# Turning the value products of three attention stages: values as weights in 32-column tiles, exponentials streamed, key sums from a block of ones

## The chip, the core and the metric

One Trainium2 chip, one core. The metric is the device time of one execution of the whole program, in microseconds (us). The program computes a four-layer decoder for 128 sequences of 64 tokens with 128 features, all in float32; what is changed lies in three of its twelve steps.

The engines are named as in the profile: PE multiplies matrices (its weight loads are listed apart, as PEld), DVE is the vector engine, ACT the scalar engine, POOL the general engine, SP starts DMAs. A matmul holds one operand (the weights, or stationary operand) and streams the other; the result goes to PSUM, a small memory of eight banks, from which DVE and ACT read.

## What is computed

The three steps are multi-head attentions with 16 heads of 8 features over 64 keys. The first, cut to what matters:

```python
qh = (q @ W_q).reshape(B, S, 16, 8); kh = (k @ W_k).reshape(...); vh = (v @ W_v + b_v).reshape(...)
scores = jnp.einsum('bihd,bjhd->bhij', qh, kh) * scale
keep = (j < i) | (i == 0) & (j == 0)
probs = jax.nn.softmax(jnp.where(keep, scores, -jnp.inf), axis=-1)
attn = jnp.einsum('bhij,bjhd->bihd', probs, vh).reshape(B, S, 128)
return attn @ W_o + b_o
```

The second adds a bias that falls with the distance of query and key (and has no bias on the values); the third masks by an input matrix, and has biases on the values and on the output. A layer normalization of x plus the result follows each. Two other attentions share the code and keep their old form: one with differential heads, one with padded keys.

## The kernel before

**Chunks.** All tokens stay in SBUF as 16 arrays X[c] of 128x4x128: a chunk c is 512 tokens, that is 8 sequences (BPC) or 4 blocks of 128 tokens (TPC). `mha` (L1160) runs an attention step as a pipeline over the chunks. Tile pools and a scheduler decide buffers and the final order on each engine; each engine works in order.

**One chunk, in two halves hf of 4 sequences.** `project` makes q and k, with features on partitions, and `expanded` copies of them in which all heads but one are zero (L1185 on ACT, L1187 on POOL and DVE). `project_v` (L1204) makes the values, with keys on partitions, and ACT copies them to VX (L1223). `scores` (L1225) multiplies queries and keys into four PSUM banks s_ps, adds the mask with matmuls (L1471, L1602), and DVE takes the maximum over the keys, four reductions m of 128x512 (L1243). `split_maxima` (L1249) splits the maxima into two bf16 parts hl, and `maxima` (L1256) turns them on PE into mT. `weights` (L1264) computes the same scores the other way round, keys on partitions, into four banks t_ps (L1273), adds the mask (L1473, L1476, L1608) and the maxima by a matmul with mT (L1285), and ACT takes the exponential into e (L1292): 128 partitions (two parities of heads by 64 keys) by 4 groups of 512 columns.

**The value products.** `values` (L1296) takes e as the weights, 64 columns for one head pair and sequence, and streams 18 columns of VX: 8 value features for each of the two heads of a pair, and two columns that hold one for the keys of the one or the other, so that the sum of the exponentials comes out beside the output (L1310). 32 such matmuls make one half. The result has queries on partitions. DVE inverts the 32 sums (L1315) and multiplies (L1324) into o, 128x4x128.

**After it.** The output projection needs features on partitions, so `transposed` (L328) turns o with four PE transposes and an ACT copy, which also adds the values' bias where there is one (L335); then four matmuls with W_o, an addition on DVE (L407), and the layer normalization (`ln_stats` L373 to L376, `rsqrt` L347 to L352, `ln_apply` L385 or L387).

**What sets the order.** The body of mha's loop (L1328 to L1363) for chunk c: `weights(c, 0)`, `load(c + 2)`, `values(c - 1, 1)`, `scores(c + 1, 0)`, the transposes of chunk c - 1, `project_v(c + 1)`, `weights(c, 1)`, `values(c, 0)`, `scores(c + 1, 1)`, `split_maxima(c + 1)`, `project(c + 2)`, the output projection of c - 1, `maxima(c + 1)`. s_ps and t_ps share a pool of five banks (psA); av_ps, oT_ps, v_ps, the q and k products, y and mT_ps share one of three (psB).

**Work put aside into the loop.** In the second step (`attn_alibi`) `rejoin` puts a row gather at each of four places of the loop: DVE copies an index column to `fat` (L1863), POOL starts an indirect DMA that adds rows to X (L1864). In the third step (`xattn_masked`) `kept` advances the planner of the last step, with matmuls, DVE and POOL work of its own. Its masks come by DMA (L1585), one of the two into a part of VX, and DVE turns them into bf16 (L1590).

**VX** are two arrays of 128x2176 for even and odd chunks. Before each attention POOL sets them to zero (L1174) and copies the ones (L1176). `cleared` uses a part of VX[0] as a source of zeros for DMAs (L2160).

Of the kernel before, what the change touches and what calls it, by code (L numbers as in the profile page):

```python
# [15 lines left out]
U8 = mybir.dt.uint8  # L16
# [6 lines left out]
P = 128  # L23
# [217 lines left out]
def tile_decoder(ctx: ExitStack, tc: tile.TileContext, a, out):  # L241
# [73 lines left out]
    def sc(n):  # L315
        return small[:, _SMALL[n][0] : _SMALL[n][1]]
# [840 lines left out]
    def rows32(t, g):  # L1157
        return t[32 * g : 32 * g + 32]

    def mha(prepare, wv, finish, mask=None, diff=False, aside=lambda c, k, seen: None):  # L1160

# [7 lines left out]
        wide_v = 2 * dh + 2  # L1169
        scale = 1.0 / math.sqrt(HD)  # L1170
        st = {}
        vxs = [v[:, : BPC * 8 * wide_v].rearrange("p (b n w) -> p b n w", b=BPC, n=8) for v in VX]
        for v in vxs:
            G.memset(v, 0.0)  # L1174
            for i in range(2):
                G.tensor_copy(v[:, :, :, 2 * dh + i], sc("vm2")[:, i : i + 1, None].to_broadcast([P, BPC, 8]))  # L1176

        def expanded(x, n, eb):

# [24 lines left out]
        def project_v(c):  # L1204
            src, vx = st[c]["src"], vxs[c % 2]
            per = dh * 8
            ps = [bank("v_ps") for _ in range(BPC * per // 512)]
            nb = 512 // per
            for b in range(BPC):
                for i in range(2):  # L1210
                    w = wv if diff else wv.rearrange("p (n i d) -> p i n d", n=8, i=2)[:, i]
                    mm(
                        ps[b // nb][i * S : (i + 1) * S, b % nb * per : (b % nb + 1) * per],
                        src[:, b * S : (b + 1) * S], w, start=True, stop=True,
                    )
            for n, v in enumerate(ps):
                for i in range(2):
                    q = slice(i * S, (i + 1) * S)
                    dst, src_ = vx[q, n * nb : (n + 1) * nb, :, i * dh : (i + 1) * dh], v[q].rearrange("p (b n d) -> p b n d", b=nb, n=8)
                    if diff and i:  # L1220
                        A.activation(dst, src_, AF.Identity, scale=nlam[q])
                    else:
                        A.copy(dst, src_)  # L1223
# [71 lines left out]

        def values(c, hf):  # L1296
            s = st[c]
            if hf == 0:
                s["o"] = work("o", (P, TPC, D))
                s["tmp"] = work("ye", (P, 2, 8, 2, 16), "dtmp") if diff else None  # L1300
            e, o, vx = s["e"][hf], s["o"], vxs[c % 2]
            ev = e.rearrange("p g (a u j q) -> p g a u j q", u=2, a=2, j=2)
            n_t = 1 if diff else 2
            for u0 in range(0, 2, n_t):
                ps = bank("av_ps")
                av = ps[:, : n_t * 8 * wide_v].rearrange("p (n w) -> p n w", w=wide_v)
                for u in range(u0, u0 + n_t):
                    for n in range(8):
                        for j in range(2):
                            mm(  # L1310
                                av[j * S : (j + 1) * S, 8 * (u - u0) + n, :], ev[:, n // 2, n % 2, u, j, :],
                                vx[:, 2 * (2 * hf + u) + j, n, :], start=True, stop=True,
                            )
                rc = sm.tile([P, 8 * n_t, 2], F32, tag=f"rc{n_t}", name="rc")
                V.reciprocal(rc, av[:, :, 2 * dh :])  # L1315
                src = av[:, :, : 2 * dh].rearrange("p n (i d) -> p n i d", i=2)
                t = 2 * hf + u0
                if diff:
                    d = s["tmp"][:, u0]
                    V.tensor_tensor(d, src, rc[:, :, :, None].to_broadcast([P, 8, 2, dh]), ALU.mult)  # L1320
                    G.tensor_tensor(o[:, t, :].rearrange("p (n d) -> p n d", n=8), d[:, :, 0, :], d[:, :, 1, :], ALU.add)
                else:
                    dst = o[:, t : t + 2, :].rearrange("p t (n i d) -> p (t n) i d", n=8, i=2)
                    return V.tensor_tensor(dst, src, rc[:, :, :, None].to_broadcast([P, 16, 2, dh]), ALU.mult).ins  # L1324

        nlam = lam_neg() if diff else None
        on, late, spread, done = range(NC), (), None, None
# [36 lines left out]
        for _ in late:  # L1364
            pass

    def out_projected(c, o, wo, bv=None, base=None, after=None, on_act=False):
        oT = transposed(o, "oT", bias=bv)
        xb = base() if base else None
        yield  # L1370
        y = bank("y")
        for t in range(TPC):
            mm(y[:, t * P : (t + 1) * P], oT[:, t * P : (t + 1) * P], wo, start=True, stop=True)
        r = added(c, y, xb)
        yield
        layernorm(c, r, on_act=on_act)
        if after:
            after(c)
# [15 lines left out]
    def attn_diff():  # L1394
# [49 lines left out]
        mha(prepare, w[:, 2, :], finish, diff=True)  # L1444
        layernorm(NC - 1, rs.pop(NC - 1))


# [38 lines left out]
    def xattn_causal():  # L1486
        w = W[4]
        cleared([(XR, 4 * P * QUADS)])
        mha(
            cross(w, None, None), w[:, 2, :],  # L1490
            lambda c, s: out_projected(c, s["o"], w[:, 3, :], bv=col("l1xbv"), base=lambda: with_bias(c, "l1xbo")),
            mask=everywhere(half[:, 128:256].rearrange("p (n h k) -> p n h k", n=2, h=1)),
        )

    def attn_alibi():
# [4 lines left out]

        def finish(c, s):
            c = order[c]
            oT = transposed(s["o"], "oT")
# [29 lines left out]
    def xattn_padded():  # L1533
# [33 lines left out]
            yield  # L1567
            layernorm(c, r)

        mha(cross(W[7], "l2xbq", "l2xbk"), W[7][:, 2, :], finish, mask=mask)  # L1570

    def xattn_masked():
        w = W[10]
# [22 lines left out]
        def mask(c, hf, s, t):  # L1596
# [12 lines left out]

        mha(  # L1610
            prepare, w[:, 2, :],
            lambda c, s: out_projected(c, s["o"], w[:, 3, :], bv=col("l3xbv"), base=lambda: with_bias(c, "l3xbo"), on_act=c > 11),
            mask=mask, aside=kept,
        )

# [541 lines left out]

    def cleared(stores):

        z = VX[0][:, BPC * 8 * 18 : BPC * 8 * 18 + D]  # L2160
        G.memset(z, 0.0)
        for x, n in stores:
            for o in range(0, n, 16 * P):
# [52 lines left out]
```

## Time and profile before

| | us |
|---|---|
| median of 8 runs (3368.92 to 3395.17) | 3379.93 |
| the profiled execution | 3382.01 |
| its span, first to last instruction | 3378.9 |

| engine | busy us | share of the span |
|---|---|---|
| PE | 2897.4 | 86% |
| PEld | 2099.2 | 62% |
| DVE | 2035.5 | 60% |
| ACT | 1620.3 | 48% |
| POOL | 1535.5 | 45% |

The mean granted clock of PE is 0.915. In the page's list of groups, L1310 is the costliest on PE: its matmuls are busy for 348.2 us and its weight loads for 328.3 us. Busy times overlap, since matmuls are pipelined: a mean of 217 ns for one does not mean one per 217 ns.

Three views are used further on. The view of stretches has a row for each stretch: from and to, length, busy time and number of instructions, granted clock, share of the DMA engines, GB/s. The timeline has a row for instructions of one kind in succession: start, duration from the first to the last, engine, line, operation, output and inputs, array tile or shape, number; in brackets the idle time before it and what ended that. The list of groups has busy time and mean duration, then the idle time before and its causes. A f32 matmul shows as two records, a weight load and a matmul each, as it takes two passes.

### The profile page before, as it was taken

The page shows a single profiled execution, that of the slowest core. Times are in us where ns is not written, and L with a number is a line of the kernel's source. Part 1 is how long each engine was busy: PE and PEld are TensorE (multiplying, and loading weights), DVE is VectorE, ACT ScalarE, POOL GpSimd, SP SyncE. Part 2 cuts the span into 40 slices and gives each one's busy share as a digit, 9 for nine tenths or more (in the row PEclk, how much of TensorE's full clock was granted, in tenths as well). Part 3 has the DMA queues.
Part 4 walks back from the last instruction along what each step waited for, and adds up shares of the span by engine and source line. Part 5 has one row for each costly group of instructions (what it writes and reads, how often), then busy time and mean ns, then how long its engine had stood idle before and what let it go on. Part 6 is the DMA issues. An engine that isn't in the chain of part 4 may idle for free. (4 is left out here: it accounts for less than half of the span.)

```text
span 3378.9 us, 110606 instructions
## 1 busy us (share of the span) xinstructions
PE 2897.4 (86%) x46690; PEld 2099.2 (62%) x46690; DVE 2035.5 (60%) x7300; ACT 1620.3 (48%) x3150; POOL 1535.5 (45%) x1543
## 2 busy tenths in 40 slices
PE   5898868998998899978788899998998669988993
PEld 3788845665666677845565677773443337766882
DVE  3732357766777666443355565667888876663345
ACT  2443346755554565322344545553545556643443
POOL 3555545234555444234455354556666224353244
PEclk9999988999999899788788889999998899996996
DMA  4577721000001000014510000000000000011684
GB/s 121 153 193 228 227 59 37 14 8 3 3 3 43 27 4 4 6 37 113 139 14 13 3 5 4 4 10 3 1 1 7 4 5 18 18 32 42 185 247 121
DMA packets 191633, 182.22 MB, mean 54 GB/s; under 512 B 30176, under 2 KB 166624, under 8 KB 191136
## 3 DMA queue, kind: packets, MB, share of 16 engines
q1 hardware_dynamic: 160688, 136.66, 13.9%
q0 software_dynamic: 20224, 32.28, 4.2%
q8 instruction: 366, 6.00, 0.7%
q10 hardware_dynamic: 10224, 6.22, 0.6%
q14 instruction: 131, 1.07, 0.1%
HBM read 132.34 MB, written 42.73 MB: 52 GB/s over the span
## 5 line engine op out<-in xcount | busy, mean ns | idle before, releaser
L1243 DVE TENSOR_REDUCE m<-s_ps 128x8 f32<-128x512 f32 x640 | 397.5, 683 | 201.4 <-PE s_ps L1471 100.3
L1292 ACT ACTIVATE e<-t_ps 128x512 f32<-128x512 f32 x640 | 329.5, 599 | 175.7 <-PE t_ps L1285 175.3
L1310 PE MATMUL av_ps<-vx,e 128*64 128x18 f32 (+1 forms) x10240 | 348.2, 217 | 14.4 <-issue 13.1
L1310 PEld LDWEIGHTS av_ps<-vx,e 128*64 128x64 f32 x10240 | 328.3, 142 | 36.6 <-issue 28.9
L792 ACT ACTIVATE hT<-h_ps,aux 128x256 f32<-128x256 f32 x496 | 204.3, 471 | 254.5 <-PE h_ps L790 137.6
L1187 POOL TENSOR_SCALAR eb<-qT,small 128x512 f32<-128x512 f32 x80 | 131.7, 1646 | 381.2 <-ACT qT L970 170.1
L1273 PE MATMUL t_ps<-eb,kT 32*64 32x128 f32 x10240 | 289.0, 287 | 7.2 <-DVE m L1243 3.3
L1235 PE MATMUL s_ps<-eb,qT 32*64 32x256 f32 x5120 | 249.9, 423 | 48.1 <-ACT e L1292 23.4
L825 POOL DMA_INDIRECT got<-l_rout,fat x192 | 192.7, 1004 | 210.6 <-DVE r L835 95.8
L790 PE MATMUL h_ps<-ebT,rw 128*128 128x256 f32 x992 | 245.9, 392 | 25.4 <-DVE ebT L778 10.1
L803 PEld LDWEIGHTS yg<-rw,hT 128*128 128x128 f32 x1984 | 244.0, 193 | 15.4 <-ACT hT L792 6.1
L803 PE MATMUL yg<-rw,hT 128*128 128x128 f32 x1984 | 246.8, 277 | 5.4 <-ACT hT L792 4.0
L1273 PEld LDWEIGHTS t_ps<-eb,kT 32*64 32x64 f32 x10240 | 203.3, 133 | 76.4 <-DVE m L1243 26.5
L387 POOL TENSOR_SCALAR x<-xb,lnmv,ln_y 128x128 f32<-128x128 f32 x200 | 157.3, 798 | 159.8 <-DVE ln_y L352 159.8
L765 POOL DMA_INDIRECT aux<-in_x_dram,rat x156 | 159.7, 1024 | 143.9 <-issue 55.4
L1315 DVE RECIPROCAL rc<-av_ps 128x32 f32<-128x32 f32 (+1 forms) x192 | 61.7, 321 | 268.6 <-PE av_ps L1310 261.5
L790 PEld LDWEIGHTS h_ps<-ebT,rw 128*128 128x128 f32 x992 | 183.7, 195 | 53.8 <-DVE ebT L778 13.7
L804 DVE TENSOR_TENSOR yo<-yg,aux 128x256 f32<-128x256 f32 x124 | 52.4, 422 | 265.9 <-PE yg L803 87.7
L1235 PEld LDWEIGHTS s_ps<-eb,qT 32*64 32x64 f32 x5120 | 126.6, 141 | 101.9 <-ACT e L1292 38.7
L1185 ACT ACTIVATE eb<-qT,small 128x512 f32<-128x512 f32 x160 | 106.8, 715 | 128.7 <-POOL qT L1412 123.8
L1187 POOL TENSOR_SCALAR eb<-kT,small 128x512 f32<-128x512 f32 x80 | 145.6, 1820 | 21.5 <-ACT kT L972 11.4
L1968 PE MATMUL ye_ps<-w_l2f,box 128*128 128x512 f32 x256 | 135.8, 649 | 0.0
(517 smaller groups left out, 6444.9 us busy)
## 6 DMA issues: line engine op xcount, KB each, us to landing
rw<-in_l0w_dram SPq DMA_DIRECT2D x78, 512.0 KB
rw<-in_l3w_dram SPq DMA_DIRECT2D x46, 512.0 KB
l_rout<-yo SPq DMA_DIRECT2D x124, 128.0 KB
aux<-xd SPq DMA_DIRECT2D x46, 128.0 KB
aux<-in_l0b_dram SPq DMA_DIRECT2D x78, 66.0 KB
xd<-vx SPq DMA_DIRECT2D x5, 1024.0 KB
plan<-xr ACTq DMA_DIRECT2D x18, 256.0 KB
yr<-plan SPq DMA_DIRECT2D x18, 256.0 KB
```

Source lines behind the costliest of these rows:

```text
L387: (V if on_dve else G).tensor_scalar(X[c][:, t, :], r[:, t, :], mv[:, t, 0:1], y[:, t : t + 1], ALU.subtract, ALU.mult)
L765: s.gather = G.indirect_dma_start(out=eb[:, i, :], out_offset=None, in_=x[:, :], in_offset=bass.IndirectOffsetOnAxis(ap=at[:, i : i + 1], ...
L790: s.pe = mm(ps[:, j * GR : (j + 1) * GR], w1[:, (k + j) * P : (k + j + 1) * P], ebT, start=True, stop=True)
L792: s.act_ins = A.activation(hT[k + j], ps[:, j * GR : (j + 1) * GR], s.act, bias=v[:, k + j : k + j + 1])
L803: s.pe = mm(y[:, i * P : (i + 1) * P], hT[k][:, i * P : (i + 1) * P], w2[:, k, :], start=(k == 0), stop=(k == FK - 1))
L825: s.gather = G.indirect_dma_start(out=got[i][k][:, t, :], out_offset=None, in_=s.rout[b][:, :], in_offset=bass.IndirectOffsetOnAxis(ap=at[ ...
L1187: ins = (G if h == 2 else V).tensor_scalar(dst, x, mine, None, ALU.mult)
L1235: mm(ps[g][j * S : (j + 1) * S, u * 256 : (u + 1) * 256].rearrange("p (h k) -> p h k", h=4), rows32(s["q"], g)[:, b], rows32(s["eb"], g)[: ...
L1243: last = V.tensor_reduce(s["m"][:, g, 2 * hf : 2 * hf + 2, :].rearrange("p t h -> p (t h)"), ps[g].rearrange("p (n k) -> p n k", k=S), AX. ...
L1273: mm(ps[g][i * S : (i + 1) * S].rearrange("p (a u j q) -> p a u j q", u=2, a=2, j=2)[:, :, u, j, :], rows32(s["k"], g)[:, b], rows32(s["eb ...
L1292: last = A.activation(e[:, g, :], ps[g], AF.Exp, scale=scale)
L1310: mm(av[j * S : (j + 1) * S, 8 * (u - u0) + n, :], ev[:, n // 2, n % 2, u, j, :], vx[:, 2 * (2 * hf + u) + j, n, :], start=True, stop=True,)
```

## The change

The new form, `turned_values`, is used with `flat=True`, in the causal, the biased and the masked attention; the other two pass `flat=False` and stay as they were.

```diff
-        vxs = [v[:, : BPC * 8 * wide_v].rearrange("p (b n w) -> p b n w", b=BPC, n=8) for v in VX]
...
+        if flat:
+            vxs = [v[:, : BPC * 4 * 48] for v in VX]
+            key_sums = VX[1][:, 2048:2096]
+            G.memset(key_sums, 0.0)
+            for v in vxs:
+                G.memset(v, 0.0)
             for i in range(2):
+                G.tensor_copy(key_sums[:, 16 + i * dh : 16 + (i + 1) * dh], sc("vm2")[:, i : i + 1].to_broadcast([P, dh]))
...
+                    if flat:
+                        A.copy(
+                            vx[q].rearrange("p (m x r) -> p m x r", x=3, r=16)[:, :, 0::2, i * dh : (i + 1) * dh],
+                            v[q].rearrange("p (m x d) -> p m x d", x=2, d=dh),
+                        )
+                        continue
...
+        def turned_values(s, hf, vx):
+
+            if hf == 0:
+                s["oT"] = work("oT")
+            ps = bank("av_ps")
+            av, total = ps[:, :256], ps[:, 256:]
+            for a_ in range(2):
+                for g in range(4):
+                    mm(
+                        total[32 * g : 32 * g + 32, :], key_sums[:, 16 - 16 * a_ : 48 - 16 * a_],
+                        s["e"][hf][:, g, a_ * 256 : (a_ + 1) * 256], start=(a_ == 0), stop=(a_ == 1), skip_group_check=True,
+                    )
+            for x in range(4):
+                for a_ in range(2):
+                    for g in range(4):
+                        at = ((4 * hf + x) * 4 + g) * 48 + 16 * a_
+                        mm(
+                            av[32 * g : 32 * g + 32, x * S : (x + 1) * S], vx[:, at : at + 32],
+                            s["e"][hf][:, g, a_ * 256 + x * S : a_ * 256 + (x + 1) * S], start=(a_ == 0), stop=(a_ == 1), skip_group_check=True,
+                        )
+            dst = s["oT"][:, hf * 256 : (hf + 1) * 256]
+            V.reciprocal(dst, total)
+            return V.tensor_tensor(dst, av, dst, ALU.mult).ins
...
+    def with_values_bias(bo, bv, wo):
+
+        ps = bank("bo_ps")
+        mm(ps[:, :D], col(bv).to_broadcast([P, P]), wo, start=True, stop=True)
+        V.tensor_tensor(row(bo), row(bo), ps[:, :D], ALU.add)
+
+    def out_projected(c, oT, wo, base=None, after=None, on_act=False):
-        oT = transposed(o, "oT", bias=bv)
...
-        used = BPC * 8 * 18
+        used = BPC * 4 * 48
+        with_values_bias("l3xbo", "l3xbv", w[:, 3, :])
...
-            m = work("t1", (P, BPC * 2 * S // 4), "mu").bitcast(U8), VX[c % 2][:, used + 512 : used + 768].bitcast(U8)
+            m = [work(n, (P, BPC * 2 * S // 4), "mu").bitcast(U8) for n in ("t1", "o")]
```

In words. The values are now the weights and the exponentials are streamed. In VX each sequence and group g of four heads has 48 columns: 16 for the first head pair (a_ = 0), 16 zeros, 16 for the second. The 32 columns from 0 or from 16 are the weights for the one or the other pair, with zeros in the place of the other, and the two products are added in PSUM. A group's output takes 32 of the 128 partitions, so the four groups fill the 128 features, and the output has features on partitions: 32 matmuls of 64 streamed columns for a half. The sums come from 8 matmuls of 256 columns with a block of ones (`key_sums`, in the same layout), so that each of the 128 output rows has its sum in the same bank, beside it. DVE inverts 128x256 sums and multiplies into oT, which the output projection takes as it is. The transposes of o and their copies are gone; the values' bias, multiplied by W_o, is added to the row of the output's bias once at the start of the step. The masks' second tile moves from VX to the buffers of tag "o", which these attentions no longer use, and the source of zeros in `cleared` moves to the end of VX[0].

More of the change, by code (lines that the diff above doesn't have):

```diff
@@ L1158, in rows32, with mha @@
         return t[32 * g : 32 * g + 32]
-    def mha(prepare, wv, finish, mask=None, diff=False, aside=lambda c, k, seen: None):
+    def mha(prepare, wv, finish, mask=None, diff=False, aside=lambda c, k, seen: None, flat=True):
         dh = 16 if diff else 8
@@ L1171, in mha @@
         st = {}
-        vxs = [v[:, : BPC * 8 * wide_v].rearrange("p (b n w) -> p b n w", b=BPC, n=8) for v in VX]
-        for v in vxs:
-            G.memset(v, 0.0)
-            for i in range(2):
-                G.tensor_copy(v[:, :, :, 2 * dh + i], sc("vm2")[:, i : i + 1, None].to_broadcast([P, BPC, 8]))
+        if flat:
[4 more added lines that the diff above has]
+                G.memset(v, 0.0)
+            for i in range(2):
+                G.tensor_copy(key_sums[:, 16 + i * dh : 16 + (i + 1) * dh], sc("vm2")[:, i : i + 1].to_broadcast([P, dh]))
+        else:
+            vxs = [v[:, : BPC * 8 * wide_v].rearrange("p (b n w) -> p b n w", b=BPC, n=8) for v in VX]
+            for v in vxs:
+                G.memset(v, 0.0)
+                for i in range(2):
+                    G.tensor_copy(v[:, :, :, 2 * dh + i], sc("vm2")[:, i : i + 1, None].to_broadcast([P, BPC, 8]))
         def expanded(x, n, eb):
@@ L1297, in values @@
             s = st[c]
+            if flat:
+                return turned_values(s, hf, vxs[c % 2])
             if hf == 0:
@@ L1365, in mha @@
             pass
-    def out_projected(c, o, wo, bv=None, base=None, after=None, on_act=False):
-        oT = transposed(o, "oT", bias=bv)
+    def with_values_bias(bo, bv, wo):
[3 more added lines that the diff above has]
+    def out_projected(c, oT, wo, base=None, after=None, on_act=False):
         xb = base() if base else None
@@ L1442, in finish @@
             rs[c] = added(c, ps)
-        mha(prepare, w[:, 2, :], finish, diff=True)
+        mha(prepare, w[:, 2, :], finish, diff=True, flat=False)
         layernorm(NC - 1, rs.pop(NC - 1))
@@ L1488, in xattn_causal @@
         cleared([(XR, 4 * P * QUADS)])
+        with_values_bias("l1xbo", "l1xbv", w[:, 3, :])
         mha(
             cross(w, None, None), w[:, 2, :],
-            lambda c, s: out_projected(c, s["o"], w[:, 3, :], bv=col("l1xbv"), base=lambda: with_bias(c, "l1xbo")),
+            lambda c, s: out_projected(c, s["oT"], w[:, 3, :], base=lambda: with_bias(c, "l1xbo")),
             mask=everywhere(half[:, 128:256].rearrange("p (n h k) -> p n h k", n=2, h=1)),
@@ L1502, in finish @@
             c = order[c]
-            oT = transposed(s["o"], "oT")
+            oT = s["oT"]
             r = with_bias(c, "l2abo")
@@ L1568, in finish @@
             layernorm(c, r)
-        mha(cross(W[7], "l2xbq", "l2xbk"), W[7][:, 2, :], finish, mask=mask)
+        mha(cross(W[7], "l2xbq", "l2xbk"), W[7][:, 2, :], finish, mask=mask, flat=False)
     def xattn_masked():
@@ L1611, in xattn_masked @@
             prepare, w[:, 2, :],
-            lambda c, s: out_projected(c, s["o"], w[:, 3, :], bv=col("l3xbv"), base=lambda: with_bias(c, "l3xbo"), on_act=c > 11),
+            lambda c, s: out_projected(c, s["oT"], w[:, 3, :], base=lambda: with_bias(c, "l3xbo"), on_act=c > 11),
             mask=mask, aside=kept,
@@ L2158, in cleared @@
     def cleared(stores):
-        z = VX[0][:, BPC * 8 * 18 : BPC * 8 * 18 + D]
+        z = VX[0][:, 2048 : 2048 + D]
         G.memset(z, 0.0)
```

## The prediction

> **What bounds the kernel now.** I read the stretches of the three stages that change, then one clean chunk of the causal stage on PE and DVE, then the same spot in the other two stages. Each attention stage runs 16 chunks, and each chunk two products of exponentials and values: A (the second half of the chunk before, L1338) and B (the first half of this one, L1348).
>
> ```profile
> 1112.00:1400.00 288.00, 275.27 (x8016) 0.99 0.02 5
> 1650.00:2005.00 355.00, 311.65 (x7902) 0.89 0.08 13
> 2760.00:3125.00 365.00, 328.69 (x8059) 0.90 0.09 27
> ```
>
> The rows are the causal, alibi and masked stages: length, PE busy time, granted clock. PE is busy 96% of the causal stage, so it looks as if only PE work counted. The chunk shows otherwise:
>
> ```profile
> 1195.85 2.05 PE L1310 MATMUL av_ps<-vx,e 128*64 128x18 f32 x64
> 1197.82 1.12 PE L1235 MATMUL s_ps<-eb,qT 32*64 32x256 f32 x32
> 1198.74 0.64 PE L1471 MATMUL s_ps<-half 32*64 32x512 bf16 x16
> 1199.31 0.65 PE L332 MATMUL oT_ps<-ident,o 128*128 128x128 f32 x4
> 1199.89 1.15 PE L1212 MATMUL v_ps<-w_l1x,ctx 128*64 128x64 f32 x32
> ```
>
> ```profile
> 1193.53 0.10 PEld L1260 LDWEIGHTS <-hl 128*128 128x128 bf16 x1 [0.65 <-DVE hl L1254]
> 1201.34 0.86 PEld L1273 LDWEIGHTS t_ps<-eb,kT 32*64 32x64 f32 x55 [0.17 <-DVE m L1243]
> ```
>
> ```profile
> 1188.30 0.36 DVE L1315 RECIPROCAL rc<-av_ps 128x32 f32<-128x32 f32 x1 [3.32 <-PE av_ps L1310]
> 1188.70 0.42 DVE L1324 TENSOR_TENSOR o<-av_ps,rc 128x256 f32<-128x256 f32 x1
> 1189.76 2.48 DVE L1243 TENSOR_REDUCE m<-s_ps 128x8 f32<-128x512 f32 x4 [0.64 <-PE s_ps L1471]
> ...
> 1197.94 0.36 DVE L1315 RECIPROCAL rc<-av_ps 128x32 f32<-128x32 f32 x1 [0.44 <-PE av_ps L1310]
> 1199.40 2.48 DVE L1243 TENSOR_REDUCE m<-s_ps 128x8 f32<-128x512 f32 x4 [0.64 <-PE s_ps L1471]
> ```
>
> Twice a chunk PE already waits for DVE: in half A for the maxima m, which free the banks that t_ps takes; in half B for hl, made of m. DVE's order in both halves is reciprocal, product, four maxima. Before the first maximum it idles 0.64 us for s_ps. That gap is all the cover that a longer reciprocal has; with the 0.08 us by which neighbouring DVE instructions overlap when neither waits (1189.76+2.48 against a next start of 1192.16), 0.72 us.
>
> **The change, part by part.** *Matmuls.* Before, 32 products stream 18 columns against 64-column weights: 1195.85 to 1197.82, 1.97 us, weight-load bound. After, 8 matmuls of 256 columns give the sums and 32 of 64 columns the values, on tiles of 32 columns, four side by side. Each f32 matmul shows as two records. s_ps has 32 such records of 256 columns on eight tiles, four rounds in 0.92 us (1197.82 to 1198.74); the sums are 16 records on four tiles, four rounds: 0.92 us. v_ps has 32 records of 64 columns on two tiles, 16 rounds in 1.08 us; the values are 64 records on four tiles, 16 rounds: at most 1.08, and 0.93 by the 58 ns between its records. Together 1.85 to 2.00 us; I take 1.87, 0.1 us less than before, on the path in both halves. That four column tiles run together is seen in the routed stage, where four products (eight records) take no longer than one's two passes and a tail:
>
> ```profile
> 1575.72 0.43 PE L1799 MATMUL hq_ps<-plan,vx 128*32 128x128 f32 x8
> ```
>
> The Trainium skill (TensorEngine Tiling (Array Packing), Performance Considerations) promises up to 4x for swapping the streamed side and tiling columns. By that rule a product would take 0.5 us, and 1.37 less than I take on 67 exposed products, and the whole would end near 3344 us. The rows above say that a round lasts as long as its streamed columns or its weight load, and that before, two tiles of 18 columns already ran side by side; after, half of every 32-column tile holds zeros, so no such factor is there to win.
>
> *Reciprocal.* It grows from 128x32 to 128x256, because the sums now stand under every output row.
>
> ```profile
> L1315 DVE RECIPROCAL rc<-av_ps 128x32 f32<-128x32 f32 x128 | 45.5, 356 | 257.8 <-PE av_ps L1310 250.8 <-remote 6.9
> L1315 DVE RECIPROCAL rc<-av_ps 128x16 f32<-128x16 f32 x64 | 16.1, 252 | 10.8 <-PE av_ps L1310 10.6
> ```
>
> Sixteen more columns cost 104 ns, 6.5 ns each, so 224 more cost 1.46 us: 1.81 us. The planner's two, of 28 and 36 columns, take 329 and 370 ns: 5.1 ns each, 1.50 us. A floor is the rate of the maxima, 621 ns for 512 columns (1.2 ns): 0.63 us. I take 1.81, whose form and operand (PSUM) are nearest.
>
> The Trainium skill has two rules here: VectorE: DVE Perf Modes, in its Walkthrough, says that the reciprocal is an iterative divide with a repeat count of 8. At the page's 0.96 GHz that would be 8.3 ns a column, 2.2 us, and the total near 3463. Its errata section's table, 120 cycles plus one per element, would give 0.39 us and no delay at all. The two rows above, 6.5 ns a column, refute the second and lie under the first.
>
> *Causal.* Each half: 1.46 less 0.72 makes m 0.74 us late; behind m on DVE stand the cast and split to hl, whose consumers are PE's transpose and then every later matmul. Less 0.1 for the matmuls: 0.64. Two halves, 15 chunks: 19 us.
>
> *Alibi.* In nine chunks a row gather follows the product. DVE copies its indices (fat), POOL starts it, and m begins only some 1.4 us after the gather's start, though by PE's timeline s_ps ended at 1816.66:
>
> ```profile
> 1815.61 0.42 DVE L1324 TENSOR_TENSOR o<-av_ps,rc 128x256 f32<-128x256 f32 x1
> 1815.95 0.15 DVE L1863 COPY fat<-pli 128x1 int32<-128x1 int32 x1
> 1817.75 2.48 DVE L1243 TENSOR_REDUCE m<-s_ps 128x8 f32<-128x512 f32 x4 [1.65 <-PE qT_ps L967]
> ```
>
> ```profile
> 1816.37 1.55 POOL L1864 DMA_INDIRECT x<-yr,fat  x1 [3.42 <-DVE fat L1863]
> ```
>
> So the idle 1.65 us is no cover: copy, gather and m all move by 1.46 in B. In A, DVE idles 5.2 us there behind ACT: nothing. 9 x 1.46 = 13; three chunks with B alone at 0.74, 2; four like causal, 8 x 0.74 = 6; matmuls -2. Sum 19. If the gather does not hold m, the 13 go.
>
> *Masked.* In eight chunks A starts behind the layernorm chain with 0.36 + 0.08 us of cover, so 1.02 late, 8 us; B has 2.2 us of idle behind the planner's matmuls: nothing. Two first chunks like causal, 3. In the last six, five products stand in back-to-back DVE work, 7. Matmuls -2. Sum 16. The transposed mask moves to tag "o", whose four loads follow the scan's release, ahead of their use by some 10 us (first t_ps 2772.55): nothing; uncovered, about one load, 2 us.
>
> *The rest.* The four oT transposes (0.58 us on PE) and ACT's copy (0.69) go, but PE then reaches t_ps earlier and waits for m longer: nothing, up to the 0.2 us it waits now. The vx copies keep 64x512 elements. The folded bias is a matmul and a 128x128 addition, twice, under 1 us each. The zeroing grows by a third of 1.06 us, against four 0.30 us copies dropped. At each stage's end the longer reciprocal stands against the dropped transposes and copy. Together +2.
>
> Sum: 19 + 19 + 16 + 2 = 56. The profiled execution took 3382.01 us (span 3378.9), 2.1 above the median 3379.93; on the median's scale 3436.
>
> **Rivals.** (1) Faster: the reciprocal costs under 0.36 + 0.72 = 1.08 us at 256 columns, which decides, and m is no later. Then matmuls gain 0.1 on some 67 exposed products (7) and dropping the transposes 0.2 on 40 chunks (8): 3365. Against it: all reciprocal rows. (2) Column tiles run only in pairs: 1.87 becomes 3.74, 1.77 more on 88 products, 155, plus 56: 3590. Against: hq_ps. (3) The delay is hidden outside causal chunks: 19 + 6 of alibi's last + 3: about 3408. For: DVE's long idle there; against: the gather's constant 1.4 us. (4) Nothing is covered, DVE's order makes all 96 products late by 1.46 less 0.1: 131, 3511. Against: the 2.2 and 5.2 us gaps. That the change doesn't do what it says is excluded by the built order: 96 products have 8 + 32 matmuls and the wide reciprocal, and the transposes are gone.
>
> **How the numbers follow.** Forecast 0.66; rivals 0.08, 0.04, 0.13, 0.09. Within the forecast, the slope of 5.1 takes 0.31 from 67 products, 21; a free gather takes 13, the planner's chunks 7: down to 3395. Low 3397; up, half of rival 4: 3475. No change is within 0.3%, about what this kernel's measurement can tell: 0.03, from the overlap of (1) and (3). Faster 0.08, slower 0.89.
>
> **What would show it.** DVE's reciprocal near 1.8 us, 96 times, DVE busy some 135 us more; no idle on DVE before m in causal; PE waiting for m and hl by 0.7 us more a half; values' records in 1.9 us; the causal stage 19 us longer with less PE busy. A reciprocal under 1.1 us, or PE gaps unchanged, would make it wrong.

## The result, and the profile after

The changed kernel takes 3396.66 us (median of 22 runs, 3385.26 to 3415.66), the kernel before 3378.37 (64 runs); the ratio is 1.0062, 95% interval 1.0047 to 1.0076. So it is slower, by 18 us where 56 were forecast, just below the forecast range. The profiled execution took 3405.45 us (span 3403.6, mean granted clock 0.927), 23.4 more than that of before.

First the stretches of PE, from the first maximum of a stage to its last. The columns are those of the prediction: from and to, length, PE busy and its instructions, granted clock, DMA share, GB/s. The rows are causal, alibi, the end of alibi (its last maxima to the padded stage's first) and masked; before:

```profile
1120.86:1379.08 258.22, 248.50 (x7471) 1.00 0.02 4
1647.53:1984.74 337.21, 296.63 (x7470) 0.89 0.09 15
1984.74:2020.93 36.19, 29.34 (x539) 0.80 0.03 8
2767.25:3081.64 314.39, 290.64 (x7551) 0.95 0.08 23
```

and after:

```profile
1118.93:1399.11 280.18, 257.19 (x7880) 0.99 0.06 17
1665.06:2001.18 336.12, 285.93 (x7884) 0.93 0.07 10
2001.18:2027.86 26.68, 23.72 (x579) 0.94 0.04 11
2775.95:3107.34 331.39, 296.04 (x7960) 0.95 0.08 21
```

Causal is 22.0 us longer (19 forecast), masked 17.0 (16 forecast). Alibi is 1.1 shorter (19 longer forecast) and its end 9.5 shorter (nothing forecast). All other stretches together are 3.7 shorter; the sum, 24.7, is the difference of the spans.

The groups of the changed kernel, with the idle time before them and its main cause:

```profile
L1258 DVE TENSOR_REDUCE m<-s_ps 128x8 f32<-128x512 f32 x640 | 396.8, 682 | 108.3 <-PE s_ps L1517 49.6
L1364 DVE RECIPROCAL oT<-av_ps 128x256 f32<-128x256 f32 x96 | 168.6, 1756 | 189.4 <-PE av_ps L1359 189.4
L1288 PEld LDWEIGHTS t_ps<-eb,kT 32*64 32x64 f32 x10240 | 214.8, 132 | 114.5 <-DVE m L1258 61.1
```

The reciprocal takes 1.756 us, 96 times (1.81 forecast). The idle time before the maxima has halved (201.4 us before): it was the cover. PE's weight loads for t_ps now wait 61.1 us for the maxima (26.5 before). DVE is busy 2169.8 us, 134 more (135 forecast).

A clean causal chunk on DVE and then on PE, start and duration of each row, in brackets the idle time and what ended it:

```profile
1205.55 1.76 DVE L1364 RECIPROCAL oT<-av_ps 128x256 f32<-128x256 f32 x1 [0.41 <-PE av_ps L1359]
1207.34 0.42 DVE L1365 TENSOR_TENSOR oT<-av_ps,oT 128x256 f32<-128x256 f32 x1
1207.68 2.47 DVE L1258 TENSOR_REDUCE m<-s_ps 128x8 f32<-128x512 f32 x4
```

```profile
1203.52 1.07 PE L1351 MATMUL av_ps<-e,vx 128*32 128x256 f32 x16
1204.41 1.08 PE L1359 MATMUL av_ps<-e,vx 128*32 128x64 f32 x64
1205.41 1.12 PE L1250 MATMUL s_ps<-eb,qT 32*64 32x256 f32 x32
```

The product is 0.89 us of sums and 1.00 of values, 1.89 together (1.87 forecast, 1.97 before). The maxima follow the product without a gap. The causal period is 18.0 to 18.8 us a chunk; before it was 16.9 in the first chunks and 17.1 to 18.2 in most later ones. Over the 13 chunks from the third on, the stage loses 16.1 us, 0.62 us a half (0.64 forecast). The excess over 19 us is in the second chunk (21.9 for 16.8), which holds two waits for instructions of 0.8 us and slower matmuls behind a wait for hl.

Half B of alibi behind a gather, where the forecast failed, on DVE and POOL:

```profile
1781.40 1.76 DVE L1364 RECIPROCAL oT<-av_ps 128x256 f32<-128x256 f32 x1 [4.07 <-PE av_ps L1359]
1783.19 0.42 DVE L1365 TENSOR_TENSOR oT<-av_ps,oT 128x256 f32<-128x256 f32 x1
1783.53 0.14 DVE L1911 COPY fat<-pli 128x1 int32<-128x1 int32 x1
1783.59 2.47 DVE L1258 TENSOR_REDUCE m<-s_ps 128x8 f32<-128x512 f32 x4
1785.98 0.87 DVE L1196 TENSOR_SCALAR eb<-qT,small 128x512 f32<-128x512 f32 x1
...
1787.48 0.57 DVE L1269 TENSOR_TENSOR hl<-m,hl 128x64 bf16<-128x64 f32 x1
```

```profile
1783.94 1.55 POOL L1912 DMA_INDIRECT x<-yr,fat  x1 [4.76 <-DVE fat L1911]
1785.01 2.30 POOL L1196 TENSOR_SCALAR eb<-qT,small 128x512 f32<-128x512 f32 x1
```

Before, the gather started first and m 1.4 us behind it, 2.53 us after the reciprocal's start. Now s_ps is done when the product ends, m starts at once, 2.19 us after the reciprocal's start, and the gather starts 0.35 us behind m. So m comes 0.34 us earlier than it did, but what follows m takes longer: from m's start to the end of hl it is 4.46 us, where it was 3.71. The same two DVE rows in the half before:

```profile
1820.15 0.48 DVE L1187 TENSOR_SCALAR eb<-qT,small 128x512 f32<-128x512 f32 x1
...
1821.25 0.21 DVE L1254 TENSOR_TENSOR hl<-m,hl 128x64 bf16<-128x64 f32 x1
```

POOL's two eb instructions take 2.30 us each beside them, where they took 1.57 and 1.79; why both engines are slower here, no run shows. From the start of the reciprocal to the end of hl it is 6.65 us, where it was 6.24: the half is 0.40 us longer, not 1.46.

### The profile page after: what moved, and what is told of

It is laid out like the page before. It is cut to its first block, busy times and chain, and to the rows that moved or that the text cites. A ratio compares the mean times of both kernels' runs of the same rounds, so it can differ in the third digit from the quotient of the medians.

```text
span 3403.6 us, 113204 instructions
## 1 busy us (share of the span) xinstructions
PE 2882.3 (85%) x48038; PEld 2029.9 (60%) x48038; DVE 2169.8 (64%) x7302; ACT 1589.1 (47%) x3102; POOL 1538.3 (45%) x1540
## 4 chain that ended last, share of the span: by engine, by line
PE 47%; DVE 31%; issue 7%; ACT 6%; POOL 5%; DMA 3%; another core or an unknown queue 1%; SPq 0%; POOLq 0%; DVEq 0%; ACTq 0%
DVE m L1258 8%; PE h_ps L790 5%; PE yg L803 5%; PE s_ps L1250 4%; PE t_ps L1288 3%; DVE oT L1364 3%; PE av_ps L1327 3%; PE av_ps L1359 2%; PE av_ps L1351 2%; PE y L1134 2%; DVE lnst L373 2%; POOL x L387 1%; PE ye_ps L2016 1%; PE t_ps L1300 1%
## 5 line engine op out<-in xcount | busy, mean ns | idle before, releaser
L1288 PE MATMUL t_ps<-eb,kT 32*64 32x128 f32 x10240 | 321.3, 287 | 25.2 <-DVE m L1258 12.8
L1364 DVE RECIPROCAL oT<-av_ps 128x256 f32<-128x256 f32 x96 | 168.6, 1756 | 189.4 <-PE av_ps L1359 189.4
L1288 PEld LDWEIGHTS t_ps<-eb,kT 32*64 32x64 f32 x10240 | 214.8, 132 | 114.5 <-DVE m L1258 61.1
L1250 PE MATMUL s_ps<-eb,qT 32*64 32x256 f32 x5120 | 241.5, 406 | 36.5 <-ACT e L1307 19.6
L1327 PE MATMUL av_ps<-vx,e 128*64 128x34 f32 (+1 forms) x4096 | 137.5, 220 | 3.7 <-issue 3.5
L1327 PEld LDWEIGHTS av_ps<-vx,e 128*64 128x64 f32 x4096 | 129.6, 140 | 12.3 <-issue 9.7
```

The costliest lines, as they stand in the source:

```text
L1250: mm(ps[g][j * S : (j + 1) * S, u * 256 : (u + 1) * 256].rearrange("p (h k) -> p h k", h=4), rows32(s["q"], g)[:, b], rows32(s["eb"], g)[: ...
L1288: mm(ps[g][i * S : (i + 1) * S].rearrange("p (a u j q) -> p a u j q", u=2, a=2, j=2)[:, :, u, j, :], rows32(s["k"], g)[:, b], rows32(s["eb ...
L1327: mm(av[j * S : (j + 1) * S, 8 * (u - u0) + n, :], ev[:, n // 2, n % 2, u, j, :], vx[:, 2 * (2 * hf + u) + j, n, :], start=True, stop=True,)
L1364: V.reciprocal(dst, total)
```

## The experiments

The runs fell on chips of two kinds. On some the kernel before takes 3360 to 3380 us, as in the result above, on others 3240; the first maximum of the first attention comes after 745 to 759 us on the former and 686 to 699 on the latter. Ratios are to the kernel before on the same chip. They are called the 3380 and the 3240 chips. Chip number 3 stands in both kinds (e5 to e8 at 3240, e13 to e16 at 3380), so whether the chips themselves differ, their machines or a state that changes with time, isn't shown.

### The long reciprocal alone, in the kernel before (e1, e15)

```diff
...
-                V.reciprocal(rc, av[:, :, 2 * dh :])
+                if wide_rc:
+                    rc = work("oT", (P, 16, 16), "rc")
+                    V.reciprocal(rc, av[:, :, 2:])
+                    rc = rc[:, :, 14:]
...
```

> The kernel before, with one thing changed: in the causal, biased and masked attentions DVE inverts 128x256 elements of av_ps where it inverted 128x32 (the 32 sums among them, which alone are used). PE's work, the transposes and the turn of the output stay as before. Theory 1 (the reciprocal's extra 1.4 us is exposed only where the scores' banks wait for DVE; behind a row gather it uses up the hold that the gather had on the maxima): causal +19 to +22 us, masked +16, the nine gather chunks of alibi about 0 in B and its last chunks +6, so +40 to +45 in all, ratio 1.012 to 1.013. Theory 2 (the prediction's: the gather moves along and holds the maxima all the same): alibi +19 to +21, in all +55 to +58, ratio 1.0165. Theory 3 (the loss comes from the new matmuls or from the instruction stream, not from DVE): within 0.3% of before.

> The kernel before with the long reciprocal alone. Theory 1 (the forecast's price of the reciprocal, 1.9%, is right in size, and what was missed is what the dropped turn gives back): 1.018 to 1.022; against the profile of before on this chip causal +17 to +20, alibi +9 to +14, masked +15 to +18. Theory 2 (the reciprocal costs less than forecast): 1.010 to 1.014.

Measured on 3380 chips: 1.0208 (1.0179 to 1.0237) and 1.0194 (1.0174 to 1.0215). The reciprocal's price in the forecast was 56 us and the 7 that the matmuls were to gain, 1.9%: right in size for the old form, and theory 1 of e15 by the total. Its place was right in part: in e15 causal is 21 us longer than in the profile of before on that chip, masked 19, alibi 12.5, and its end 9. These are rough, as the profile of e15 fell on its longest execution (3461 us, granted clock 0.901) and also has 21 us more between causal's last maxima and alibi's first, where next to nothing was changed; from the first profile of before to e1 they are 19, 10, 10 and 3.5. The total is above what any theory of e1 expected; alibi is near theory 1, though not 0 in its B halves. DVE's rows of such a half, in e1:

```profile
1674.71 1.76 DVE L1316 RECIPROCAL rc<-av_ps 128x256 f32<-128x256 f32 x1 [4.09 <-PE av_ps L1310]
...
1676.90 2.47 DVE L1243 TENSOR_REDUCE m<-s_ps 128x8 f32<-128x512 f32 x4
```

As in the changed kernel, m follows the product without a gap and no longer waits behind the gather: the gather's hold and the reciprocal do not add up.

### The changed kernel with a short reciprocal (e2), and a square of four (e9 to e12)

```diff
-            V.reciprocal(dst, total)
-            return V.tensor_tensor(dst, av, dst, ALU.mult).ins
+            rc = sm.tile([P, 32], F32, tag="rc2", name="rc")
+            V.reciprocal(rc, total[:, :32])
+            return V.tensor_tensor(..., rc[:, None, :].to_broadcast([P, 8, 32]), ALU.mult).ins
```

It inverts 32 of the 256 columns of sums and scales every query by one of these, so its outputs are not the attention's; it serves only to price the reciprocal. The square has a long or a short reciprocal, without the turn (the transposes and their copy) or with it. The turn kept as dead work, at the start of what follows each chunk's product:

```diff
+    def turned_again(oT):
+        ps = bank("oT_ps")
+        for t in range(TPC):
+            nc.tensor.transpose(ps[:, t * P : (t + 1) * P], oT[:, t * P : (t + 1) * P], ident)
+        A.copy(work("o"), ps)
```

> The changed kernel, but DVE inverts only the first 32 of the 256 columns of sums, and every query of a half is scaled by one of these 32, so the outputs of the three attentions are scaled by other queries' sums. All matmuls, the dropped transposes and the second product on DVE stay. Theory 1: without the long reciprocal m is no later than before; the matmuls' 0.1 us on some 67 exposed products (7) and what the dropped transposes give at the stages' ends (12 in the one profile) are left: 3355 to 3370 us, ratio 0.993 to 0.998; and in alibi's B halves the maxima start about 1.4 us behind the gather's start again, as before, so that alibi gains no more than in the changed kernel. Theory 2 (the gather holds the maxima however early they could start): the gather chunks of alibi are 1.4 us shorter than in the changed kernel. Theory 3 (the new matmuls cost it): still 1.004 to 1.007.

> The changed kernel with the dropped work put back as dead work: after each first half of the three attentions PE turns the finished oT with four transposes into a bank and ACT copies it to a buffer that nobody reads. Theory 1 (in the biased attention's half A, PE comes out of its wait for ACT late and is itself the bound, so four transposes of 0.6 to 0.7 us lie on the path; in the causal one they fill PE's wait for the maxima): alibi +8 to +11 us against the changed kernel, its end +5 to +9, causal 0 to +2, masked 0 to +4, so 13 to 25 in all and 1.010 to 1.014 of the kernel before. Theory 2 (the prediction's: worth nothing, up to 0.2 us a chunk): 1.005 to 1.0085, as the changed kernel.

> The changed kernel itself once more, as the first corner of a square of four (long or short reciprocal, with or without the turn of the output) on one chip. 1.0047 to 1.0076 of the kernel before, as in its own measurement.

> Second corner: long reciprocal, turn kept as dead work (the same kernel as the run that kept the turn). Theory 1 (the turn is worth far more beside the long reciprocal, because its transposes then also wait for the late product): 1.016 to 1.022, against 1.006 without the turn. Theory 2 (the prediction's: the turn is worth nothing): within 0.3% of the first corner.

> Third corner: the short reciprocal (128x32, so the outputs of the three attentions are scaled by other queries' sums), no turn: 0.991 to 0.996, as in its own run.

> Fourth corner: the short reciprocal (outputs scaled by other queries' sums) and the turn kept as dead work; beside the kernel before it differs by the products alone. Theory 1 (the turn is cheap here, because the product comes early, and dear beside the long reciprocal): 0.996 to 1.000, so the turn is worth 0.3 to 0.6% here and 1.0 to 1.4% in the other pair. Theory 2 (turn and reciprocal add up): 1.003 to 1.008, 1.0 to 1.4% above the third corner as well. Theory 3 (the new products themselves cost or gain more than 0.3%): outside of 0.997 to 1.003.

> The changed kernel with the turn kept as dead work. If before takes 3380 us here: theory 1 (the turn gives back more there) 1.016 to 1.021, like before with the long reciprocal; theory 2 (the products give back more there) 1.009 to 1.013. If before takes 3240 us: 1.019 to 1.025 as in the two runs before.

> Short reciprocal (outputs scaled by other queries' sums), new products, turn kept as dead work. If before takes 3380 us here: theory 1 (the products are worth nothing on either machine) 0.998 to 1.002; theory 2 (they are worth more there) 0.990 to 0.996. If before takes 3240 us: 0.998 to 1.002 as in the square.

e2, on a 3380 chip, gave 0.9934 (0.9910 to 0.9958), and in its B halves m is again 1.34 us behind the gather's start: theory 1. All others fell on 3240 chips, where the changed kernel loses more than in its first measurement, so the ranges of e5 and e9, made from that, were too low (e17 came out below its range of 1.019 to 1.025):

| | without the turn | turn kept |
|---|---|---|
| long reciprocal | e9 1.0153 (1.0127 to 1.0179) | e10 1.0225 (1.0195 to 1.0254), e5 1.0193 (1.0160 to 1.0225), e17 1.0171 (1.0138 to 1.0203) |
| short reciprocal | e11 0.9953 (0.9928 to 0.9978) | e12 1.0000 (0.9976 to 1.0024), e18 0.9997 (0.9974 to 1.0020) |

e12 and e18 differ from the kernel before by the products, their copies and what goes with these (the layout of VX, the folded bias): streaming the exponentials in 32-column tiles is worth no more here than the runs can tell, some 0.2%. The reciprocal costs 2.0% in both columns (with the mean of the three, 1.0196, in the right one; 2.0, 2.2 and 1.7% between runs on one chip). The turn costs 0.5% beside the short reciprocal and 0.4% beside the long one by that mean, 0.7% on the one chip that has both corners: some 15 us, up to 25. So on these chips they add up within the spread. Theory 1 of e12 fits its own corner, but not the other pair, where the turn was to be worth 1.0 to 1.4%. The forecast had priced the turn at nothing.

On the 3380 chips they do not add up. From e2 to the changed kernel (1.0050 to 1.0062) the reciprocal costs 1.2 to 1.3% in the new form, where it costs 1.9 to 2.1% in the old one (e1, e15). By stages, from e2's profile to those of the changed kernel (e14's among them), causal and masked are 18 us longer each, alibi only 5 to 7 and its end 3 to 4 shorter.

Where does the turn lie on the path? At the end of alibi, which takes 25.4 us in e9 and 36.4 in e10. PE there, in e10:

```profile
1926.60 0.44 PE L1417 MATMUL oT_ps<-ident,oT 128*128 128x128 f32 x2 [2.11 <-DVE oT L1365]
1926.88 0.92 PE L1563 MATMUL y<-w_l2a,oT 128*128 128x128 f32 x4
1927.59 1.06 PE L332 MATMUL xT_ps<-ident,x 128*128 128x128 f32 x4
```

and in e9:

```profile
1923.74 0.71 PE L1555 MATMUL y<-w_l2a,oT 128*128 128x128 f32 x4
1924.29 0.60 PE L332 MATMUL xT_ps<-ident,x 128*128 128x128 f32 x4
```

With the turn, PE stands 2.11 us for the product of the last half before it may turn it, and the next stage's xT stands behind. Without it PE takes xT at once, and the last y fits in later. The first xT comes 20.2 us into the stretch in e10 and 15.3 in e9, 4.9 of the 11 us; the rest comes behind it, where the first q and k products take nearly twice as long in e10 and PE then waits 4.45 us ahead of s_ps.

In alibi's half A the turn is on the path too. PE there in the kernel before, and then the changed kernel:

```profile
1804.74 2.53 PE L1235 MATMUL s_ps<-eb,qT 32*64 32x256 f32 x25 [2.21 <-ACT e L1292]
...
1808.48 0.74 PE L332 MATMUL oT_ps<-ident,o 128*128 128x128 f32 x4
1809.15 1.15 PE L1212 MATMUL v_ps<-w_l2a,xT 128*64 128x64 f32 x32
1810.23 1.32 PE L1273 MATMUL t_ps<-eb,kT 32*64 32x128 f32 x59
```

```profile
1795.72 2.53 PE L1250 MATMUL s_ps<-eb,qT 32*64 32x256 f32 x25 [1.93 <-ACT e L1307]
...
1799.46 1.23 PE L1221 MATMUL v_ps<-w_l2a,xT 128*64 128x64 f32 x32
1800.61 1.91 PE L1288 MATMUL t_ps<-eb,kT 32*64 32x128 f32 x59
```

PE comes out of its wait for ACT late and then runs without a gap up to t_ps: no wait for m is there that could swallow the 0.67 us. With the turn kept beside the long reciprocal, alibi is 5.1 to 7.0 us longer (e10, e17 and e5 against e9).

### Both kernels on one 3380 chip (e13, e14), and what differs between the chips

No edit in either; both ran on the same chip.

> The kernel before, unedited, for its profile beside the next two on one chip. Ratio 1. Theory 1 (the first profile of before was slow in alibi, at a low clock): alibi 312 to 322 us on a chip whose runs of before take 3240 us, and 10 to 16 below the changed kernel's. Theory 2 (the change gains in alibi): alibi 328 to 338, as long as the changed kernel's.

> The changed kernel again. Theory 1 (the size of the loss goes with the chip's granted clock: where before is granted 0.93 the loss is 1.5%, where it is granted 0.915 it is 0.6%): 1.013 to 1.018 on a chip that runs before in 3240 us, 1.004 to 1.008 on one that takes 3380. Theory 2 (the first measurement or the second was off by chance): the same ratio on either, near 1.010.

The kernel before gave 1.0003 of itself (0.9984 to 1.0022), the changed one 1.0050 (1.0027 to 1.0073). So 0.5 to 0.6% on the 3380 chips and 1.5% on the 3240 chip are both real; theory 1 of e14 fits, theory 2 falls. Alibi takes 337.3 and 338.0 us (its end 35.2 and 25.2), as in the first pair and as theory 2 of e13 has it: the first profile of before was no bad draw for such a chip. On the 3240 chip it takes 328.5 in e9, and 316.0 in e12. The lines of B in e11 say why the short reciprocal is that much faster there:

```profile
1708.33 0.36 DVE L1365 RECIPROCAL rc<-av_ps 128x32 f32<-128x32 f32 x1 [4.21 <-PE av_ps L1359]
...
1709.06 0.14 DVE L1912 COPY fat<-pli 128x1 int32<-128x1 int32 x1
1709.79 2.49 DVE L1258 TENSOR_REDUCE m<-s_ps 128x8 f32<-128x512 f32 x4 [0.58 <-PE s_ps L1518]
```

```profile
1709.47 1.54 POOL L1913 DMA_INDIRECT x<-yr,fat  x1 [3.52 <-DVE fat L1912]
```

The gather starts 0.32 us ahead of m and does not hold it: m starts 0.02 us after the last s_ps matmul. The same kernel on a 3380 chip (e2) has m 1.34 us behind the gather and 1.07 behind s_ps:

```profile
1822.04 2.48 DVE L1258 TENSOR_REDUCE m<-s_ps 128x8 f32<-128x512 f32 x4 [1.61 <-PE qT_ps L967]
```

```profile
1820.70 1.56 POOL L1913 DMA_INDIRECT x<-yr,fat  x1 [3.77 <-DVE fat L1912]
```

From reciprocal to hl it is 5.17 us here and 6.21 there with the short one, and 6.65 on either with the long one. So the long reciprocal costs 1.48 us in such a half on the 3240 chips and 0.44 on the 3380 chips; over the eight B halves behind a gather, whose s_ps is not always as early, it is 10.8 us (e11 to e9) and 3.6 (e2 to the changed kernel). That is 7 us of the some 30 by which the losses differ (1.53% of 3242 against 0.62% of 3378). Of the 1.48 us, m is late by 0.73 (2.19 us behind the reciprocal's start for 1.46), and the other 0.75 is again the longer way from m to hl.

### The gathers moved behind the maxima, in the kernel before (e6)

```diff
-            aside(c, 0, (behind, done, spread))
             seen = scores(c + 1, 0) if c + 1 in on else None
+            aside(c, 0, (behind, seen or done, spread))
...
-            aside(c, 2, (done, spread))
...
             seen = maxima(c + 1) if c + 1 in on else None
+            aside(c, 2, (seen or done, spread))
```

> The kernel before, unchanged but for the place of the row gathers of the biased attention: where they stood behind the product of half A and of half B, they now stand behind the maxima of half A and behind the copy of mT. Theory 1 (the gather's start ahead of the maxima is what held them, and its place is what made alibi 47 us shorter in the run with the normalization behind the maxima): alibi 290 to 310 us instead of 337, ratio 0.984 to 0.993. Theory 2 (that gain needed the new products and the later normalization): alibi 325 to 337, ratio 0.996 to 1.001.

1.0016 (0.9996 to 1.0036): theory 2. It ran on a 3240 chip, where by e11 and e12 the gather holds nothing to begin with (in the new form; the kernel before has no profile there); whether it would gain on a 3380 chip wasn't measured.

### The new form in alibi alone (e4, e7)

```diff
-            mask=everywhere(half[:, 128:256]...),
+            mask=everywhere(half[:, 128:256]...), flat=False,
```

and likewise for the masked attention, each with its old finish and buffers.

> The new form in the biased attention (alibi) alone; the causal and masked attentions are as before the change. Theory 1 (the long reciprocal costs nothing there, because the maxima now start ahead of the gather, and the stage's end gains from the dropped transposes): alibi and its two ends give the -13 us that the profile of the changed kernel shows, 3362 to 3372 us, ratio 0.995 to 0.998. Theory 2 (the prediction's account of alibi): +19, ratio 1.0055. Theory 3 (the gain at the ends is the clock's, not the kernel's): ratio 0.999 to 1.002.

> The new form in the biased attention alone; the causal and masked attentions are the kernel before's, with the transposes in their old place. Theory 1 (alibi and its ends give the -13 us that the profile of the changed kernel shows; the loss is the causal and the masked stage's): 0.994 to 0.998 of before. Theory 2 (the prediction's account, +19 in alibi): 1.0055.

e4 gave 0.9942 (0.9922 to 0.9962), but in its two old attentions o is turned ahead of the second half's product, so it is not the comparison that was meant. e7 has the old order: 0.9989 (0.9968 to 1.0011) on a 3240 chip, between the two theories. In alibi and its end, cost and gain nearly cancel there.

### Reciprocal and product behind the maxima (e3, e8, e16)

```diff
+            def normalize():
+                V.reciprocal(dst, total)
+                return V.tensor_tensor(dst, av, dst, ALU.mult).ins
+            return normalize
...
+            seen = scores(c + 1, 0) if c + 1 in on else None
+                    with tc.issue_after(seen) if seen else nullcontext():
+                        done = done()
...
             seen = maxima(c + 1) if c + 1 in on else None
+                    with tc.issue_after(seen) if seen else nullcontext():
+                        done = done()
```

The gathers that follow the product move with it. e3 has it in all three attentions, e8 in alibi with the two others as before the change, e16 in causal and alibi with masked as before.

> The changed kernel with the same instructions, but reciprocal and product are held back on DVE: in half A behind the four maxima of the next scores, in half B behind the maxima, their split and the copy of mT. Theory 1 (the loss is the reciprocal's place ahead of the maxima): m starts as soon as s_ps is there, the causal period returns from 18.3 to 16.5 to 16.9 us a chunk and masked likewise; in alibi the gather no longer stands ahead of m: 3330 to 3365 us, ratio 0.985 to 0.996. Theory 2 (DVE has no room, or the av_ps bank, one of three, kept longer, holds up the next products): no better than the changed kernel, ratio 1.003 to 1.012.

> The new form in the biased attention alone, with reciprocal and product behind the maxima (and the gathers behind those); the causal and masked attentions are the kernel before's. Theory 1 (the run with all three in this form gained 47 us and 10 at the end of alibi, lost 2 in causal and 15 in masked): 15 us below that run, ratio 0.980 to 0.985, the best of all so far. Theory 2 (masked's loss in that run is the planner's and not the form's): no better than that run, 0.985 to 0.989.

> The new form with reciprocal and product behind the maxima in the causal and the biased attention; the masked one is the kernel before's. Theory 1 (the later place is worth 1.3% in alibi and nothing in causal, and masked loses in the new form): 0.984 to 0.988, as with alibi alone. Theory 2 (the causal stage gains too, since its m is no longer late and the turn is gone): 0.980 to 0.984.

Measured: e3 0.9867 (0.9841 to 0.9894), e8 0.9866 (0.9834 to 0.9899, on a 3240 chip), e16 0.9821 (0.9796 to 0.9847). All beat both kernels, and e16 has the lowest ratio; e8 is in the range of its theory 2. From the third chunk on the causal period is back at 16.8 to 18.0 us, but the stage, 262.5 us in e16, does not gain against 256.9 (e13): theory 2 of e16 has the right number for another reason. The new form does cost masked something: 329.0 us in e3, 313.0 in e16 and 316.9 before, all on 3380 chips. Most of e16's gain, 44 of some 62 us, is in alibi, 293.2 us against 337.3, and 8 more at its end; on the 3240 chip alibi goes from 331.1 in e7 to 289.9 in e8, which differs by the later place (the gathers' too) alone. It isn't the maxima alone: PE's wait for hl shrinks by 9 us there (e13 to e16). ACT's rows in an A half of e6, which keeps the old order, and of e3:

```profile
1698.05 1.65 ACT L385 ACTIVATE x<-x,lns,rms_y 128x128 f32<-128x128 f32 x4 [4.36 <-DVE lns L382]
1699.60 2.02 ACT L1292 ACTIVATE e<-t_ps 128x512 f32<-128x512 f32 x4
```

```profile
1726.04 1.58 ACT L1307 ACTIVATE e<-t_ps 128x512 f32<-128x512 f32 x3 [0.69 <-PE t_ps L1300]
1731.53 1.65 ACT L385 ACTIVATE x<-x,lns,rms_y 128x128 f32<-128x128 f32 x4 [3.91 <-DVE lns L382]
1733.08 0.57 ACT L1307 ACTIVATE e<-t_ps 128x512 f32<-128x512 f32 x1
```

In the old order the layer normalization of the rejoined rows stands ahead of all four exponentials, and the exponentials' banks, which s_ps needs, come free late. Here DVE reaches the normalization later, and the scheduler puts three exponentials ahead of it: PE's wait for ACT moves from s_ps (23.4 us in e13) to t_ps (17.6 in e16), PE is busy for 34 us less (293.8 and 259.7), and the granted clock of the stage is 0.96 where it was 0.90. So what the later place was meant for, in causal, only undid the delay, and alibi's 44 us, 1.3%, go with ACT's order and the higher clock. That ACT's order is the cause, and alone would do it in the kernel before, is argued from these rows and wasn't tried.

## Why the prediction was wrong

- *Matmuls*: 1.89 us for 1.87. The 0.1 us a half, some 7 us in all or 0.2%, is less than e12 and e18 can tell from nothing. The Trainium skill (TensorEngine Tiling (Array Packing), Performance Considerations) lists 4x column tiling for such a swap; with 1.97 us before and e12 at 1.0000, no gain of that size shows in this kernel.
- *Reciprocal*: 1.756 us for 1.81. Its price over the whole, 1.9%, was confirmed in the old form (1.9 to 2.1%, e1 and e15) and on the 3240 chips (1.7 to 2.2%); in the new form on the 3380 chips, where the forecast was put to the test, it is 1.2 to 1.3%, some 40 us for 63, and most of what it lacks is in alibi. The Trainium skill's repeat count of 8 (VectorE: DVE Perf Modes, Walkthrough), by the prediction's estimate 8.3 ns a column at the page's clock, is above the 6.25 ns that the two widths give ((1756 - 356) / 224).
- *Causal*: 19 forecast, 22.0 measured (22.5 on another chip, e13 to e14). Mechanism and size right, but for the second chunk's 5 us, which weren't forecast.
- *Masked*: 16 forecast, 17.0 (14.6 there). Right, in its mechanism too: in the eight A halves behind the layer normalization m starts 2.13 us behind the reciprocal's start, where it was 1.16 (1.02 late forecast), and the B halves there are no longer than before. The late chunks shift by several us in either direction.
- *Alibi, the step that failed first*: "the idle 1.65 us is no cover: copy, gather and m all move by 1.46 in B". They do not move together. What holds m is a gather that starts while m waits for s_ps; the longer reciprocal lets s_ps finish first, so m goes ahead of the gather and even starts 0.34 us earlier than before. The 0.40 us a half that took the place of 1.46 (some 3 us that of 13) is the slower work between m and hl, which the forecast did not have. The alternative in the text, "if the gather does not hold m, the 13 go", was the wrong way round as well: on the 3240 chips the gather holds nothing, and 11 of the 13 are paid. That this is near the forecast is luck: half of it is m's lateness of 0.73 us, as in a half without a gather, and half the slower work behind m.
- *The turn, the step that failed second, and by more*: "nothing, up to the 0.2 us it waits now", and at the stages' ends "the longer reciprocal stands against the dropped transposes and copy". That was read off the causal chunk, where PE waits for m, and carried to places where it doesn't. In alibi PE waits for ACT ten times, and 0.67 us of turn stood behind each, 7 us (5.1 to 7.0 where the turn was kept); its end is 9.5 us shorter. With the 3 for the gather halves, 0.77 us in each of the seven B halves without one (5.95 us from reciprocal to hl for 5.18) and the forecast's 2 for the matmuls, which no run shows, alibi comes by this estimate to 3 + 5 - 7 - 2 = -1, near the -1.1 and +0.7 measured. It leaves out three A halves near the stage's end in which m is 0.7 us later, so it holds to some 2 us.
- *Rival 3* (hidden outside the causal chunks, 3408) was nearest in time, but not in cause: masked is not hidden, and alibi is paid back rather than covered.

On the 3240 chip the loss is 50 us (0.0153 of 3242): 65 for the reciprocal, 2.0%, less 15 for the turn. There the total of the gather halves is near the forecast's, by luck, and the turn was mis-sized all the same.

What stays open: on the 3380 chips the products and the dropped turn together give back 1.4% (1.0194 and 1.0208 with the long reciprocal alone, 1.0050 and 1.0062 for the change), with the short one 0.7% (e2), and on the 3240 chips 0.4 to 0.7%. The granted clocks go with it: medians 0.9085 in e15, 0.916 before and 0.9255 in e14 on one 3380 chip, 0.929 before and 0.933 in e9 on the 3240 chip. Whether the clock is the cause or follows from PE's shorter waits, no run separates; the corners with the turn kept all ran on 3240 chips. So that the turn paid back alibi on the 3380 chips rests on the rows of PE and on its end (9.5 and 10.0 us shorter there, 11 longer with the turn kept here), not on a run with the turn kept there.

## What to carry to other kernels

Price removed work stage by stage, as added work is: four transposes were free where the engine waited for something else, and dear behind another wait and at a stage's end, where nothing covers. Two delays that end in the same instruction cover each other; ask what a later start lets finish first before adding them up, and follow the chain to its last instruction: here m came earlier and hl later. And when a reordering wins, look at every engine's order for the reason: here the gain went with ACT's, which nobody had touched.

## What the runs showed of the hardware

- A gather on POOL that starts while DVE waits for PE put DVE's next instruction at 1.33 to 1.41 us after the gather's start on the 3380 chips (before, e2, e13; up to 1.6 where s_ps itself ended late), and not on the 3240 chips (e11, e12, e18: 0.02 us after PE's last matmul). Maxima already running beside the gather kept their 2.47 us for four.
- After a wait of about 2 us PE's next matmuls ran at a lower granted clock: 0.61 in the 2.5 us behind the 1.93 us wait of the changed kernel, 1.00 ahead of it; 25 of s_ps took 2.53 us there, 32 take 1.12 elsewhere. Such a wait is paid a second time. The stretches, columns as above:

```profile
1790.50:1793.00 2.50, 2.07 (x80) 1.00 0.01 3
1795.70:1798.20 2.50, 2.48 (x35) 0.61 0.00 0
```

- One and the same program ran 4% apart on the two kinds of chip (3378 and 3242 us), with some 65 us of it ahead of the first attention, and the change's ratio differed by 0.9%. A ratio of one per cent belongs to where it was measured as well as to the kernel.
